# Halving the last image's layer 1 convolution and scores twice

## The chip, the core and the metric

The kernel runs on one core of a Trainium2 chip. The core has a matrix engine (TensorE, "PE" in the profile), a vector engine (VectorE, "DVE"), an activation engine (ScalarE, "ACT"), a general engine (GpSimd, "POOL") and a queue engine that issues most of the transfers (SyncE, "SP"). The metric is the time of one execution on the device in microseconds; a version is measured several times and its median is given.

## What is computed

Two attention layers follow each other on 8 images of 512 channels and 32 x 32 = 1024 tokens, all in float32. The part that matters here is layer 1, which has one head over all 512 channels:

```python
xn = group_norm(x, gamma, beta)
q = conv1x1(xn, q_w, q_b).reshape(b, c, h * w).transpose(0, 2, 1)
k = conv1x1(xn, k_w, k_b).reshape(b, c, h * w)
v = conv1x1(xn, v_w, v_b).reshape(b, c, h * w).transpose(0, 2, 1)
attn = softmax(einsum('bqc,bck->bqk', q, k) * scale, axis=-1)
out = einsum('bqk,bkc->bqc', attn, v).transpose(0, 2, 1).reshape(b, c, h, w)
return x + conv1x1(out, p_w, p_b)
```

Layer 0 has the same form with eight heads of 64 channels. Its output x is layer 1's input.

## The kernel before

**Layer 1 in the kernel.** The query and key weights are multiplied together once, at the start, into a matrix `m`, and the value and output weights into `z`. For an image with normalized input h, the kernel then computes g = m h + `ubias` (a 512 x 512 by 512 x 1024 product, "the convolution"), the scores as the product of h and g (1024 x 1024), the exponentials e of the scores, the sums of e over the keys, z h by token, and the values, z h times e, divided by the sums and added to x.

**Halving.** Each large product is cut into halves in both directions, and the 8 block products are replaced by 7 (the scheme of Strassen in Winograd's form). The blocks to be multiplied are sums and differences of the halves: `left_sums` and `right_sums` make them with 8 half-tile additions each. `wino` runs the seven products in the order 1, four in the middle, then 4 and 3. Each product is a step of four matmuls with 512 columns. The last two steps are not run at once: they go into the list `tail`, and `finish` runs them after the first step of whatever product comes next. So the end of one product and the beginning of the next always overlap on TensorE.

**Halving twice.** For the keys, queries, g and scores of most images each of the seven products is itself cut in halves: 7 x 7 quarter products with 256 columns. `inner_factors` makes the inner sums of h, four GpSimd subtractions for each of the seven (28 in all); `query_factors` does the same for a factor of g (28 in all over the seven); the inner sums of the weights are made once, at the start, by `keep2` and are stored as `sums2_m`. `conv2` runs the convolution in four groups of one or two products (2, 2, 1, 2), `scores1_twice` the scores in seven. Both use `inner_steps` for the seven steps of each: the first step's result is copied inside PSUM by ScalarE, later steps add to it, and VectorE and ScalarE combine the results into output tiles. Where three parts of an output must be added, GpSimd adds them.

**Images in turn.** The main loop runs attention 0 of image b, then products of image b - 1's layer 1 mixed with image b + 1's layer 0. So layer 1 of images 0 to 6 is done inside the loop and is halved twice: there `inner_factors` is called before the projection of image b, well ahead of its use. Layer 1 of image 7 comes after the loop, where nothing of another image is left but the last two steps of image 6's values. It is halved once: `layer1_scores` gets `inner` as None and calls `conv`, and `layer1_rest` calls `scores1`. The normalized h of image 7 is loaded and scaled during image 6's values (the list `ahead`).

**What else hangs on it.** In the loop, group-norm statistics of the image that was just projected (`stats`) are run between the score products, on VectorE. After the loop the list is empty. `scores1` lets VectorE add up e and make the factors of e for the values; `scores1_twice` gives the totals (`add_up`) and the last four of eight subtractions for the values to GpSimd.

**Weights.** Weights are loaded through a pool of three buffers in the order of the list `uses`; `load_weight` issues the next load. A once-halved weight is one load of 1,792 KB; a twice-halved one comes in two, of 1,792 and 1,344 KB. `keep` stores the once-halved sums of a weight to memory (`sums_m` for m), `keep2` the twice-halved ones.

**Order.** Matmuls are pinned to the order of the program, as are some vector operations (`keep_in_program_order`); the rest is placed by a scheduler with its own priorities. Each engine runs its queue in order. Image-sized tiles share one pool of 32 buffers, so a new tile may have to wait for the last reader of an old one.

The names in the profile: `psa_g`, `psb_g`, `psc_g` are PSUM tiles of the convolution; `psa_sc` and the like are those of once-halved scores, and plain `psa`, `psb`, `psc` those of twice-halved ones; `inner_h` are inner sums of h, `inner` those of g, `t_h` and `sg` the outer sums of h and g; `psa_z` and `psa_av` belong to z h and the values.

Of the kernel before, what the change touches and what calls it, by code (L numbers as in the profile page):

```python
# [11 lines left out]
AF = mybir.ActivationFunctionType  # L12
# [3 lines left out]
P = 128  # L16
# [13 lines left out]
def two_attention_blocks_kernel(  # L30
# [145 lines left out]
    def main_path(ctx):  # L176
# [8 lines left out]
        def big_tile(name, shape=(P, T)):  # L185
            return big.tile(list(shape), F32, tag="big", name=name)

        def pair_tile(name):
            return big_tile(name, (P, 2, HT))
# [121 lines left out]
        uses = ["v", "p", *twice["k"], *twice["q"]] if B > 1 else ["p"]  # L311
        for b in range(1, B):
            uses += ["p", *twice["m"], "z"] + (["v", *twice["k"], *twice["q"]] if b + 1 < B else [])
        uses += ["m", "z"]
        loaded = []

        def load_weight():
# [331 lines left out]
            return scaled  # L649


        def scores1(b, gf, hf, uid):

            e = [big_tile(f"e_{uid}_{s}") for s in range(NS)]
            total = pair_tile(f"sum_{uid}")
            flat = total.rearrange("p a b -> p (a b)")
            scale = C**-0.5
            halves = lambda t: (t[:, :HT], t[:, HT:])
            ef = {p: [] for p in range(1, 8)}
            def part(j):  # L660

                def mm(p, i, ps, start):
                    for k in range(2):
                        matmul(
                            ps, hf[p][k][:, ts(2 * j + i, P)], gf[p][k], start=start and k == 0, stop=k == 1, skip_group_check=True
                        )

                def done(i, r, c, ps, u):
                    s = 4 * c + 2 * j + i
                    dst = e[s][:, ts(r, HT)]  # L670
                    if u is None:
                        nc.scalar.activation(dst, ps, AF.Exp, scale=scale)
                    else:
                        nc.vector.tensor_add(dst, ps, u)
                        nc.scalar.activation(dst, dst, AF.Exp, scale=scale)

                    if (r, c) == (1, 0):
                        if s == 0:
                            background.append(lambda: nc.gpsimd.tensor_copy(flat, e[0]))
                        else:  # L680
                            background.append(lambda: nc.vector.tensor_add(flat, flat, e[s]))
                    elif (r, c) == (0, 1):
                        background.append(lambda: nc.vector.tensor_add(flat, flat, e[s]))
                        if i == 1:
                            t = [pair_tile(f"t{n}_{uid}_{j}") for n in (1, 2, 4)]
                            fs, steps = right_sums(
                                [halves(e[2 * j + n]) for n in range(2)], [halves(e[4 + 2 * j + n]) for n in range(2)],
                                [lambda n, t=t: t[:, n, :] for t in t], nc.vector.tensor_sub,
                            )
                            for p in fs:  # L690
                                ef[p] += fs[p]
                            background.extend(steps)


                wino(f"sc_{uid}_{j}", mm, done, middle=(6, 2, 5, 7) if j else (2, 5, 6, 7))

            for j in range(2):
                part(j)
            return total, ef

        def scores1_twice(b, f, gf, gsteps, first, uid, stats):

# [158 lines left out]
        def prologue():  # L861
            raw_k = raw("k", 5)
            raw_q = raw("q", 4)
            h0 = [load_x(0, c, "h0") for c in range(KC)]
            first = {n: prepare(n) for n in "vqk"}
            wk = natural(raw_k, "k", ("a", "b"))
            wq = natural(raw_q, "q", ("c", "acc"))
            norm = GroupNorm(0, "0_0", pinned=True)
            for c in range(KC):
                norm.stats(c, h0[c])  # L870
            hf, steps = image_factors(h0, "h0_0")

# [24 lines left out]
            keep2("k", first["k"][0])  # L897
            t, steps = prepare("m")
            k = conv(weight_factors(first["k"][0]), hf, pcols("bk0"), "k0_0", hooks=[[], [], [], [], steps])
            finish()  # L900
            keep("m", t)
            keep2("m", t)
            raw_p0 = raw("p0", 3)
            wv = natural(raw_v, "v", "bc")
            norm1.group_mean(acc_tile("gmean_0_1")[:, :KC])
            product(wv, raw_p, "z")
            norm1.affine(acc_tile("gvar_0_1")[:, :KC])
            bias = bias_products([(wk, "bq1"), (raw_p, "bv1"), (raw_p0, "bv0")])
# [101 lines left out]
            q = conv2("q", f, pcols("bq0"), f"q0_{b}", hooks)  # L1010
            return q, k

        def layer1_scores(b, hf, inner, hooks=()):
            if inner:
                g = conv2("m", inner, ubias, f"g1_{b}", hooks)
            else:
                after = [load_weight, lambda: background.extend(gsteps)]
                g = conv(weight("m"), hf, ubias, f"g1_{b}", middle=(2, 5, 6, 7), back=4, after=after)
            stiles = [pair_tile(f"sg{i}_{b}") for i in (1, 2, 4)]
            halves = lambda t: (t[:, :HT], t[:, HT:])  # L1020
            gf, gsteps = left_sums(
                [halves(t) for t in g[:2]], [halves(t) for t in g[2:]],
                [lambda j, t=t: t[:, j, :] for t in stiles], nc.vector.tensor_add, nc.vector.tensor_sub,
            )
            return gf, gsteps

        def layer1_rest(b, hf, inner, gf, gsteps, stats, hooks, ahead):
            if inner:
                first = query_factors(gf[1], f"1_1_{b}")
                total, ef = scores1_twice(b, inner, gf, gsteps, first, f"1_{b}", stats)  # L1030
            else:
                total, ef = scores1(b, gf, hf, f"1_{b}")
            state = {}

            def sums():
# [16 lines left out]
        for b in range(B):  # L1052
# [33 lines left out]
            if b > 0:  # L1086
# [2 lines left out]
                for f in sums2:  # L1089
                    f()  # L1090
                norm1, stats = projection(b, af, xt, [scaled, steps[7]])
                gf, gsteps = layer1_scores(b - 1, hf, inner)
                _, _, mean, affine = norm_hooks(norm1, f"1_{b}")
                if b + 1 < B:
                    h, loads, applies = begun(load_x, norm0, b + 1, "h0")
                else:
                    h, loads, applies = begun(load_again, norm1, b, "h1")
                ahead = [loads, *([f] for f in applies)]
                layer1_rest(b - 1, hf, inner, gf, gsteps, stats, [[], mean, [], affine], ahead)
                if b + 1 < B:  # L1100
                    hf, steps = image_factors(h, f"h0_{b + 1}")
                    background.extend(steps)
# [18 lines left out]
                for f in loads + applies:  # L1121
                    f()
        hf, steps = image_factors(h, f"h1_{B - 1}")
        background.extend(steps)
        gf, gsteps = layer1_scores(B - 1, hf, None)
        layer1_rest(B - 1, hf, None, gf, gsteps, [], [[]] * 4, ())
        finish()


# [193 lines left out]
```

## Time and profile before

| | us |
|---|---|
| median of 3 runs | 2852.84 |
| lowest and highest | 2851.77, 2853.81 |
| the profiled execution, its time | 2852.44 |
| the profiled execution, its span | 2850.6 |

| engine | busy us | share of the span |
|---|---|---|
| TensorE, matmul | 2834.5 | 99% |
| TensorE, weight load | 1665.7 | 58% |
| VectorE | 2062.8 | 72% |
| ScalarE | 919.9 | 32% |
| GpSimd | 1106.2 | 39% |

The profile is of one execution. Its span goes from the first to the last instruction; the execution's own time is 1.84 us longer. A line of a timeline gives start and duration in us, engine, line of the code, operation, output tile <- input tiles, shape and the number of records; a float32 matmul of the code leaves two records. Durations of matmuls overlap a little, so the distance between two starts is the better measure. In the stretch from 2684.40 to 2773.69 us, which holds image 7's convolution and scores, TensorE is busy for 89.29 us, VectorE for 46.67, ScalarE for 15.02 and GpSimd for 1.56. In the stretch from 2553.07 to 2628.14, which holds those of image 6, they are busy for 74.88, 56.56, 23.01 and 58.01 us.

### The profile page before, as it was taken

How to read it: one execution, taken by the hardware profiler on the slowest of the kernel's cores; microseconds unless marked ns; L12 is line 12 of the kernel's file. 1: busy time of each engine (PE TensorE's matmuls, PEld its weight loads, DVE VectorE, ACT ScalarE, POOL GpSimd, SP SyncE). 2: the span in 40 equal slices, each digit the busy share in tenths (PEclk: the TensorE clock that was granted, in tenths of full speed). 3: DMA queues.
4: the chain of work that ended last, by engine and by line, in shares of the span. 5: the costliest groups of instructions: out<-in, count | busy, mean ns of one | idle time of the engine just before them, and what ended most of it. 6: DMA issues, size and time to landing. Idle time of an engine off the chain costs nothing.

```text
span 2850.6 us, 32020 instructions
## 1 busy us (share of the span) xinstructions
PE 2834.5 (99%) x11720; PEld 1665.7 (58%) x11720; DVE 2062.8 (72%) x2718; ACT 919.9 (32%) x1166; POOL 1106.2 (39%) x1110
## 2 busy tenths in 40 slices
PE   9999999999999999999999999999999999999999
PEld 5435635866367653677537674376833858348544
DVE  5587787766877678776787757877588775887654
ACT  1252452214522145221552215421163312533110
POOL 2113225732167322673127711377114761147100
PEclk9999999999999999999999999999999999999999
DMA  8722403133032231322213231122411224022201
GB/s 276 246 97 90 179 20 134 37 144 126 20 144 76 100 123 42 118 94 97 112 46 111 93 138 72 49 107 101 154 52 45 107 108 153 16 74 79 96 0 68
DMA packets 91594, 281.02 MB, mean 99 GB/s; under 512 B 10595, under 2 KB 36387, under 8 KB 82470
## 3 DMA queue, kind: packets, MB, share of 16 engines
q1 hardware_dynamic: 89638, 276.61, 26.5%
q10 hardware_dynamic: 1792, 2.29, 0.2%
q8 instruction: 95, 1.56, 0.2%
q14 instruction: 69, 0.57, 0.1%
HBM read 225.93 MB, written 52.93 MB: 98 GB/s over the span
## 4 chain that ended last, share of the span: by engine, by line
PE 98%; issue 1%; DVE 1%; POOL 0%; ACT 0%; DVEq 0%; POOLq 0%
PE sc L67 16%; PE av L67 16%; PE psb_av L67 6%; PE psb L67 5%; PE psa_av L67 4%; PE psc_av L67 4%; PE psc L67 3%; PE psa L67 3%; PE psb_z L67 3%; PE psb_p L67 3%; PE psb_v L67 3%; PE psb_g L67 3%; PE psb_k L67 3%; PE psb_q L67 2%; PE psa_p L67 2%; PE psa_z L67 2%
## 5 line engine op out<-in xcount | busy, mean ns | idle before, releaser
L625 DVE TENSOR_TENSOR sum<-sum,e 128x1024 f32<-128x1024 f32 x384 | 521.0, 1357 | 40.7 <-DVE sum L623 0.5
L621 ACT ACTIVATE e<-sc 128x1024 f32<-128x1024 f32 x512 | 476.8, 1053 | 73.4 <-PE sc L67 72.6
L67 PE MATMUL sc<-q,k 64*128 64x512 f32 x2048 | 458.7, 596 | 0.5
L67 PE MATMUL av<-e,v 128*64 128x512 f32 x2048 | 453.6, 595 | 0.0
L67 PEld LDWEIGHTS sc<-q,k 64*128 64x128 f32 x2048 | 193.2, 186 | 239.2 <-ACT e L621 104.0
L67 PEld LDWEIGHTS av<-e,v 128*64 128x64 f32 x2048 | 141.4, 137 | 304.3 <-issue 304.3
L588 POOL TENSOR_TENSOR all_recs<-all_recs,rc 128x256 f32<-128x256 f32 x72 | 63.5, 882 | 579.6 <-DVE rc L586 572.0
L644 POOL TENSOR_TENSOR a<-a,r 128x512 f32<-128x512 f32 x56 | 108.8, 1943 | 260.8 <-DMA r<-rows 246.5
L586 DVE RECIPROCAL rc<-sums 128x256 f32<-128x256 f32 x72 | 126.4, 1756 | 47.8 <-PE sums L67 26.6
L532 POOL TENSOR_TENSOR k<-k,k 128x256 f32<-128x256 f32 x28 | 20.0, 726 | 314.5 <-DVE u_k L527 314.5
L639 ACT COPY a<-av 128x512 f32<-128x512 f32 x64 | 37.4, 585 | 322.7 <-PE av L67 322.7
L623 DVE TENSOR_TENSOR sum<-e,e 128x1024 f32<-128x1024 f32 x64 | 78.4, 1226 | 59.3 <-ACT e L621 59.3
L67 PE MATMUL psa_av<-e,z 128*128 128x512 f32 x256 | 113.3, 595 | 0.0
L140 ACT ACTIVATE h<-h,b,s 128x1024 f32<-128x1024 f32 x62 | 78.5, 1270 | 87.2 <-DMA h<-in_x 70.6
L67 PE MATMUL psb<-inner,inner_h 128*128 128x256 f32 x392 | 101.6, 382 | 0.8
L411 POOL TENSOR_TENSOR inner_h<-h,inner_h 128x256 f32<-128x256 f32 x112 | 101.1, 905 | 2.2
L67 PEld LDWEIGHTS psb<-inner,inner_h 128*128 128x128 f32 x392 | 73.3, 190 | 14.9 <-POOL inner L426 3.4
L67 PEld LDWEIGHTS psa_av<-e,z 128*128 128x128 f32 x256 | 48.0, 190 | 57.3 <-issue 56.6
L411 POOL TENSOR_TENSOR inner_h<-h 128x256 f32<-128x256 f32 x56 | 55.4, 990 | 66.8 <-ACT h L140 66.8
L411 POOL TENSOR_TENSOR inner_h<-t_h 128x256 f32<-128x256 f32 x84 | 73.6, 879 | 10.8 <-PE psc_av L67 9.5
L67 PE MATMUL psb_g<-inner_h,w_m 128*128 128x256 f32 x294 | 75.1, 383 | 0.3
L67 PE MATMUL psb_q<-inner_h,w_q 128*128 128x256 f32 x294 | 75.4, 385 | 0.0
(382 smaller groups left out, 5435.2 us busy)
## 6 DMA issues: line engine op xcount, KB each, us to landing
x<-in_x SPq DMA_DIRECT2D x36, 512.0 KB
h<-in_x SPq DMA_DIRECT2D x32, 512.0 KB
spill<-x SPq DMA_DIRECT2D x32, 512.0 KB
h<-spill SPq DMA_DIRECT2D x32, 512.0 KB
x<-spill SPq DMA_DIRECT2D x32, 512.0 KB
out<-x SPq DMA_DIRECT2D x64, 256.0 KB
w_p<-sums_p SPq DMA_DIRECT2D x8, 1792.0 KB
r<-rows SPq DMA_DIRECT2D x112, 128.0 KB
```

The costliest lines, as they stand in the source:

```text
L67: tc.keep_in_program_order(nc.tensor.matmul(*args, **kw))
L140: tc.keep_in_program_order(nc.scalar.activation(dst, src, AF.Identity, bias=b, scale=s))
L411: pin(nc.gpsimd.tensor_tensor(dst, x, y, ALU.subtract))
L532: nc.gpsimd.tensor_tensor(d, x, y, ALU.add)
L586: nc.vector.reciprocal(rc, sums)
L588: nc.gpsimd.tensor_tensor(all_recs, all_recs, rc, ALU.add)
L621: nc.scalar.activation(e, sc, AF.Exp, scale=(C // 8) ** -0.5)
L623: nc.vector.tensor_add(total, es[0], e)
L625: nc.vector.tensor_add(total, total, e)
L639: nc.scalar.copy(dst, av)
L644: nc.gpsimd.tensor_tensor(dst, dst, r, ALU.mult)
```

## The change

Image 7's convolution and scores take the twice-halved path, as the other images' do. The once-halved function `scores1` goes, and `scores1_twice` takes its name; `layer1_scores` and `layer1_rest` lose their second branch. After the loop `inner_factors` is called for image 7, its GpSimd operations placed by the scheduler and not pinned, and both the outer and the inner sums of h are called for at once instead of being put in the background list. The list of weight loads has the two parts of m in the place of its once-halved form. The once-halved sums of m are no longer stored, as nobody reads them.

```diff
-        uses += ["m", "z"]
+        uses += [*twice["m"], "z"]
...
-        def scores1(b, gf, hf, uid):
...
-        def scores1_twice(b, f, gf, gsteps, first, uid, stats):
+        def scores1(f, gf, gsteps, first, uid, stats):
...
-            keep("m", t)
             keep2("m", t)
...
-        def layer1_scores(b, hf, inner, hooks=()):
-            if inner:
-                g = conv2("m", inner, ubias, f"g1_{b}", hooks)
-            else:
-                after = [load_weight, lambda: background.extend(gsteps)]
-                g = conv(weight("m"), hf, ubias, f"g1_{b}", middle=(2, 5, 6, 7), back=4, after=after)
+        def layer1_scores(b, inner):
+            g = conv2("m", inner, ubias, f"g1_{b}")
...
-            if inner:
-                first = query_factors(gf[1], f"1_1_{b}")
-                total, ef = scores1_twice(b, inner, gf, gsteps, first, f"1_{b}", stats)
-            else:
-                total, ef = scores1(b, gf, hf, f"1_{b}")
+            first = query_factors(gf[1], f"1_1_{b}")
+            total, ef = scores1(inner, gf, gsteps, first, f"1_{b}", stats)
...
         hf, steps = image_factors(h, f"h1_{B - 1}")
-        background.extend(steps)
-        gf, gsteps = layer1_scores(B - 1, hf, None)
-        layer1_rest(B - 1, hf, None, gf, gsteps, [], [[]] * 4, ())
+        inner, sums2 = inner_factors(hf, f"h1_{B - 1}")
+        for f in steps + sums2:
+            f()
+        gf, gsteps = layer1_scores(B - 1, inner)
+        layer1_rest(B - 1, inner, gf, gsteps, [], [[]] * 4, ())
         finish()
```

More of the change, by code (lines that the diff above doesn't have):

```diff
@@ L649, in attention0 @@
             return scaled
-        def scores1(b, gf, hf, uid):
[L654 to L672, printed above, removed]
-                    else:
[L674 to L679, printed above, removed]
-                        else:
[L681 to L691, printed above, removed]
-                            background.extend(steps)
[L695 to L699, printed above, removed]
-        def scores1_twice(b, f, gf, gsteps, first, uid, stats):
+        def scores1(f, gf, gsteps, first, uid, stats):
             scale = C**-0.5
@@ L1011, in keys_and_queries @@
             return q, k
-        def layer1_scores(b, hf, inner, hooks=()):
-            if inner:
-                g = conv2("m", inner, ubias, f"g1_{b}", hooks)
-            else:
-                after = [load_weight, lambda: background.extend(gsteps)]
-                g = conv(weight("m"), hf, ubias, f"g1_{b}", middle=(2, 5, 6, 7), back=4, after=after)
+        def layer1_scores(b, inner):
+            g = conv2("m", inner, ubias, f"g1_{b}")
             stiles = [pair_tile(f"sg{i}_{b}") for i in (1, 2, 4)]
@@ L1025, in layer1_scores, with layer1_rest @@
             return gf, gsteps
-        def layer1_rest(b, hf, inner, gf, gsteps, stats, hooks, ahead):
-            if inner:
-                first = query_factors(gf[1], f"1_1_{b}")
-                total, ef = scores1_twice(b, inner, gf, gsteps, first, f"1_{b}", stats)
-            else:
-                total, ef = scores1(b, gf, hf, f"1_{b}")
+        def layer1_rest(b, inner, gf, gsteps, stats, hooks, ahead):
+            first = query_factors(gf[1], f"1_1_{b}")
+            total, ef = scores1(inner, gf, gsteps, first, f"1_{b}", stats)
             state = {}
@@ L1091, in main_path @@
                 norm1, stats = projection(b, af, xt, [scaled, steps[7]])
-                gf, gsteps = layer1_scores(b - 1, hf, inner)
+                gf, gsteps = layer1_scores(b - 1, inner)
                 _, _, mean, affine = norm_hooks(norm1, f"1_{b}")
@@ L1098, in main_path @@
                 ahead = [loads, *([f] for f in applies)]
-                layer1_rest(b - 1, hf, inner, gf, gsteps, stats, [[], mean, [], affine], ahead)
+                layer1_rest(b - 1, inner, gf, gsteps, stats, [[], mean, [], affine], ahead)
                 if b + 1 < B:
@@ L1123, in main_path @@
         hf, steps = image_factors(h, f"h1_{B - 1}")
-        background.extend(steps)
-        gf, gsteps = layer1_scores(B - 1, hf, None)
-        layer1_rest(B - 1, hf, None, gf, gsteps, [], [[]] * 4, ())
+        inner, sums2 = inner_factors(hf, f"h1_{B - 1}")
[3 more added lines that the diff above has]
+        layer1_rest(B - 1, inner, gf, gsteps, [], [[]] * 4, ())
         finish()
```

## The prediction

> **What bounds the kernel now.** I read the page first (busy times, then the chain that ended last), then TensorE's timeline over the last image, then the same work for the image before it, which already runs in the changed form, then VectorE and GpSimd at the seam.
>
> ```profile
> span 2850.6 us, 32020 instructions
> PE 2834.5 (99%) x11720; PEld 1665.7 (58%) x11720; DVE 2062.8 (72%) x2718; ACT 919.9 (32%) x1166; POOL 1106.2 (39%) x1110
> ...
> PE 98%; issue 1%; DVE 1%; POOL 0%; ACT 0%; DVEq 0%; POOLq 0%
> ```
>
> TensorE (PE) is busy 99% of the span and is 98% of the chain, at full granted clock. Only fewer or cheaper matmuls can shorten the run, as long as no other engine makes PE wait. So the question is what the last image's stage costs PE now, and what it will cost. Now (timeline of PE; start, duration, tiles, records):
>
> ```profile
> 2684.40 3.60 PE L67 MATMUL psa_g<-h,w_m 128*128 128x512 f32 x8
> 2687.84 7.03 PE L67 MATMUL psb_av<-t,z 128*128 128x512 f32 x16
> 2694.70 7.03 PE L67 MATMUL psc_av<-e,sz 128*128 128x512 f32 x16
> 2701.57 3.60 PE L67 MATMUL psa_g<-h,w_m 128*128 128x512 f32 x8
> ...
> 2763.37 3.62 PE L67 MATMUL psa_z<-w_z,h 128*128 128x256 f32 x16
> ...
> 2773.69 3.62 PE L67 MATMUL psb_z<-w_z,t_h 128*128 128x256 f32 x16
> ```
>
> The convolution and the scores lie between 2684.40 and 2773.69, 89.29 us. Two steps of the previous image's values (7.03 each, 6.87 start to start) and one of z (3.45) lie among them; 89.29 - 13.73 - 3.45 = 72.11 us is the stage itself. Each step is eight records, four matmuls of the code, in 3.433 us: 858 ns for a 128x512 matmul. There are no holes. The image before, in halves twice:
>
> ```profile
> 2553.07 0.59 PE L67 MATMUL psa_g<-h,w_m 128*128 128x256 f32 x2
> ...
> 2626.41 1.03 PE L67 MATMUL psc<-inner,t_h 128*128 128x256 f32 x4
> 2627.27 1.03 PE L67 MATMUL psb<-g,inner_h 128*128 128x256 f32 x4
> 2628.14 3.62 PE L67 MATMUL psb_z<-w_z,t_h 128*128 128x256 f32 x16
> ```
>
> Its steps of two 128x256 matmuls start every 0.863 us (2626.41 to 2627.27; 0.8633 over the regular run around it), so 431.7 ns a matmul. The whole: 75.07 us, less two steps of the projection (6.87) and one of z (3.45), is 64.75 us.
>
> **What the Trainium skill says.** "FP8 and Floating Point Precision", TensorE Precision Notes: true FP32 takes four passes through the array. "TensorE: Matmul & The Clock Gate", Step-by-step: a pass streams one column a cycle at 2.4 GHz plus about 2.5 ns. An estimate from both is 4 x (512/2.4 + 2.5) = 863 ns and 4 x (256/2.4 + 2.5) = 437 ns; the trace has 858 and 432, so splitting a matmul in two costs only some 5 ns, and the product count decides. "SBUF — State Buffer", Who interferes with whom: a VectorE instruction with two SBUF inputs and a GpSimd instruction that reads SBUF exclude each other. The trace agrees: VectorE's 128x512 subtractions take 0.64 us alone (1.28 for two) and 1.17 beside GpSimd (2.34 for two, below).
>
> **Part 1: fewer products.** Removed: 7 products x 4 matmuls for the convolution and 2 x 7 x 4 for the scores, 84 x 0.8584 = 72.11 us. Added: 49 matmuls for the convolution (7 steps x (2+2+1+2) products) and 49 steps x 2 = 98 for the scores, 147 x 0.4317 = 63.45 us. On PE alone: -8.66 us.
>
> **Part 2: what the new hand-overs cost PE.** The image before spent 64.75 us against 63.45 of pure matmul: 1.30 us of waiting, some 0.4 in the convolution (2553.07 to 2582.36, less two projection steps and one score step, is 21.56; 49 matmuls are 21.15) and 0.9 in the scores. The latter sits at 2590.99 to 2599.65, where VectorE had run three group-norm statistics (1.87 us from 2583.42) ahead of the sums of g, and GpSimd stood 2.56 us for `sg` before it could make the third product's inner sums. The last image has no next image's statistics (its list is empty), so those sums come about 2 us sooner. I keep the 0.4 us and take 0.3 for the scores: +0.7. Bounds: 0 (all hidden) and 1.3 (as before it).
>
> **Part 3: the inner sums of h (28 GpSimd operations) and the seam.** They are new, ahead of everything else in GpSimd's queue, and stand in the previous image's values, where GpSimd is idle now after 2652. h is ready at 2663.6 to 2667.4. 28 x 0.9 us (the mean of those groups on the page is 879 to 990 ns) is 25 us, so they end near 2691; their tiles' old readers are all among values matmuls that end by 2677. The convolution's first use of an inner sum follows the two values steps, at 2684.40 + 0.86 + 13.73 = 2699.0. 8 us of cover: cost 0; without it, each us late is a us of PE. The eight VectorE sums of h run beside them now, each up to 0.53 us longer, and behind them stands `u_av`, whose end PE needs at 2677.54 (it ends at 2674.99 now, after 2.10 us of idleness). The same collision exists already, where an image's layer 0 sums meet the previous values (timelines of VectorE, PE and GpSimd):
>
> ```profile
> 2324.22 2.34 DVE L172 TENSOR_TENSOR h<-h,h 128x512 f32<-128x512 f32 x2
> 2326.49 2.34 DVE L173 TENSOR_TENSOR t_h<-h,t_h 128x512 f32<-128x512 f32 x2
> 2328.75 0.68 DVE L238 TENSOR_TENSOR u_av<-psb_av,t_av 128x512 f32<-128x512 f32 x1
> ...
> 2329.96 7.03 PE L67 MATMUL psb_av<-e,z 128*128 128x512 f32 x16
> 2342.12 1.52 POOL L411 TENSOR_TENSOR inner_h<-t_h,inner_h 128x256 f32<-128x256 f32 x2
> ```
>
> `u_av` ends at 2329.43, 0.5 us ahead of the matmul that needs it, and PE runs on. There h came 5.56 us after the second psa_av step began, here 5.43. So 0, with 0.5 us of slack; bounds 0 and 2.2 (13 two-input operations x 0.53 = 6.9, less the 4.65 us in hand: VectorE is free at 2672.20, and a start at 2676.85 is early enough).
>
> **Part 4: after the scores.** Twice-halved scores hand the totals, and four of the value sums, to GpSimd. The image before has this too: its total is done at 2636.5, PE asks for it at 2642.5; its last value sum at 2652.1, wanted at 2687.8. From psb_z to the end of the corresponding values steps PE took 56.26 us there and takes 55.82 here; the difference is the two group-norm matmuls, which the last image lacks. The closing check of the reciprocals now waits for GpSimd's last value sums and has z's additions queued behind it on VectorE; I place it some 2.6 us ahead of the first of these. Cost 0, bounds 0 and 1.
>
> **Part 5: memory traffic.** One 1,792 KB store of the once-halved m goes from the start; the last image's m comes in two loads (1,792 and 1,344 KB) and z's weight one load later, after the old z weight's last use (2656.9) and needed at 2763. On SP's queue the store's absence moves the load of v's weight ahead of image 1's h loads, so these have as many bytes before them as now (1,792 KB less, 1,792 more) and go out about 3 us later. ScalarE applied the first at 129.19 without waiting and has until about 133.6 (the copy at 134.91 less 1.30). Nothing else that PE reads early depends on it. Cost 0, bounds 0 and 1.
>
> **Sum.** -8.66 + 0.7 = -7.96 us. Against the profiled execution (2852.44: span 2850.6 and 1.84 around it) that is 2844.5; the median of the runs shown lies 0.4 above that execution, so 2844.9.
>
> **The rivals.**
> A, the forecast: PE keeps nearly all of the saving. For it: 98% of the chain and no holes in either form. 2844.9, its own range 2843.5 to 2846.2 (waits of 0 to 1.3, and about 0.7 us of scatter).
> B, waits between engines take a larger part: the last image stalls like the one before (1.3) and loses as much again, because the next matmul of each product waits for a ScalarE copy or a VectorE sum of the one just ended. For: each product needs PE, ScalarE, VectorE in turn. Against: the other images bear more load with 1.3. -8.66 + 2.6 = -6.1: 2846.8.
> C, the collision at the seam: the price above, 2.2, plus the 0.7: -5.8: 2847.0; a late h would add to it, to 2849.
> D, slower: the load of v's weight, ahead of h on a saturated queue (240 to 440 GB/s from 97 to 145 us), delays h, and ScalarE, which runs in order, holds the next exponentials. Every us past 133.6 is lost; it must arrive after 141.5 to make the kernel slower at all, after 147 for 0.2%. An arrival at 147 gives 133.6 to 147 less the saving, 5.5 us more: 2858. Against: the byte count ahead is unchanged.
> That the saving isn't there at all is excluded by the instruction order, which has the 147 matmuls.
>
> **How the numbers follow.** A 0.71, B 0.17, C 0.09, D 0.03. One measurement of this kernel can tell about 0.2%, 5.7 us, from no change: faster means below 2847.1. A gives all its 0.71, B about 0.11, C 0.02: 0.84. D gives 0.03 slower; 0.13 is left within. The range 2843.0 to 2848.2 holds A, B and most of C; what is left out is D, the late h in C, and scatter.
>
> **What would show it.** Right: g and score steps of 128x256 at 0.863 us, 64 us of stage, the z step's psb_z some 8 us earlier than 2773.69, the rest displaced by the same. Part 2 is wrong if the stage takes 65.5 or more; part 3 if PE has a hole before psb_av<-e,z near 2677 or before the first psb_g near 2699; part 4 if there is one before sums or the psa_av steps of the last image; part 5 if the first scores of the run shift. The forecast falls if the stage's saving and the span's differ by over 1 us.

## The result, and the profile after

| | before | after |
|---|---|---|
| median, us (20 runs each) | 2852.68 | 2848.70 |
| lowest and highest | 2851.47, 2854.32 | 2847.18, 2849.99 |
| profiled execution, its span | 2852.44, 2850.6 | 2849.52, 2847.7 |
| ratio, 95% interval | | 0.9984, 0.9978 to 0.9991 |

The changed kernel is 4.0 us faster, where 7.9 were forecast. The gain is real (the interval ends below 1), but small: 0.14% by the medians, 0.16% by the ratio, below the 0.2% that I had named as what one measurement can tell. 2848.70 lies 0.5 us above the range.

The page of the changed kernel, first its span and engines, then the engines' shares of the chain that ended last:

```profile
span 2847.7 us, 32456 instructions
PE 2827.0 (99%) x11846; PEld 1690.0 (59%) x11846; DVE 2083.8 (73%) x2733; ACT 929.0 (33%) x1177; POOL 1205.4 (42%) x1193
...
PE 97%; DVE 2%; issue 1%; ACT 0%; POOL 0%; DVEq 0%; POOLq 0%; ACTq 0%
```

PE has 7.5 us less to do (2834.5 to 2827.0), the span only 2.9. PE's busy time says that the saving is there; the rest of the page doesn't say where it went. PE's timeline over the last image does:

```profile
2686.92 0.59 PE L67 MATMUL psa_g<-h,w_m 128*128 128x256 f32 x2
...
2701.52 1.03 PE L67 MATMUL psb_g<-inner_h,w_m 128*128 128x256 f32 x4
...
2727.34 1.03 PE L67 MATMUL psc<-inner,h 128*128 128x256 f32 x4
2728.83 1.13 PE L67 MATMUL psb<-g,inner_h 128*128 128x256 f32 x4 [0.47 <-DVE e L671]
2729.80 1.03 PE L67 MATMUL psb<-inner,inner_h 128*128 128x256 f32 x4
```

And where it ends, from the same view:

```profile
2768.81 3.62 PE L67 MATMUL psb_z<-w_z,t_h 128*128 128x256 f32 x16
```

Three things are to be read here. The stage takes 81.89 us from psa_g to psb_z; less the same two values steps and one z step (17.18) it is 64.71 where the kernel before had 72.11: 7.40 saved. But psa_g starts at 2686.92, 2.52 us *later* than before (2684.40): something was lost ahead of the change. And psb_z starts 4.88 us earlier, while the span is only 2.9 shorter: 2 us more were lost behind it. I laid the starts of all of PE's rows in both traces side by side. They drift apart in steps, where PE stops in one trace and not in the other: by 0.79 at 179 us, by 1.06 at 955, by 0.36 at 1200, and by some 0.1 at each of three later places. Behind the stage PE keeps its 4.88 us to its last matmul; the rest goes between VectorE's last operation and the end of the span, 4.95 us before and 6.93 after.

### The profile page after: what moved, and what is told of

It reads as the page before. It is cut to its first block, busy times and chain, and to the rows that moved or that the text cites. A ratio compares the mean times of both kernels' runs of the same rounds, so it can differ in the third digit from the quotient of the medians.

```text
span 2847.7 us, 32456 instructions
## 1 busy us (share of the span) xinstructions
PE 2827.0 (99%) x11846; PEld 1690.0 (59%) x11846; DVE 2083.8 (73%) x2733; ACT 929.0 (33%) x1177; POOL 1205.4 (42%) x1193
## 4 chain that ended last, share of the span: by engine, by line
PE 97%; DVE 2%; issue 1%; ACT 0%; POOL 0%; DVEq 0%; POOLq 0%; ACTq 0%
PE sc L67 16%; PE av L67 16%; PE psb_av L67 6%; PE psb L67 5%; PE psa_av L67 4%; PE psc_av L67 4%; PE psc L67 3%; PE psa L67 3%; PE psb_z L67 3%; PE psb_p L67 3%; PE psb_v L67 3%; PE psb_k L67 3%; PE psb_g L67 3%; PE psb_q L67 2%; PE psa_p L67 2%; PE psa_z L67 2%
## 5 line engine op out<-in xcount | busy, mean ns | idle before, releaser
L67 PE MATMUL psb<-inner,inner_h 128*128 128x256 f32 x448 | 116.1, 382 | 1.2 <-DVE u L671 0.5
L411 POOL TENSOR_TENSOR inner_h<-h,inner_h 128x256 f32<-128x256 f32 x120 | 106.8, 892 | 2.2
L67 PEld LDWEIGHTS psb<-inner,inner_h 128*128 128x128 f32 x448 | 83.9, 190 | 16.9 <-POOL inner L426 3.8
L685 POOL TENSOR_TENSOR sum<-sum,e 128x1024 f32<-128x1024 f32 x32 | 76.2, 2380 | 27.5 <-ACT e L681 26.2
L67 PE MATMUL psb_g<-inner_h,w_m 128*128 128x256 f32 x336 | 86.0, 383 | 0.3
```

The source lines that it names most:

```text
L67: tc.keep_in_program_order(nc.tensor.matmul(*args, **kw))
L411: pin(nc.gpsimd.tensor_tensor(dst, x, y, ALU.subtract))
L685: on = lambda dst, x, y: lambda: tc.keep_in_program_order(nc.gpsimd.tensor_tensor(dst, x, y, ALU.add))
```

## What happened at the start

PE's waits in the first 260 us have one line that the kernel before hasn't:

```profile
PE sums L67 <- DVE sum L625: 0.7, 1, 0.7
```

SP's timeline, before the change (start, time in the queue's hands, DMA):

```profile
117.77 0.37 SPq L840 DMA_DIRECT2D product_z<-prodz  x1
118.69 1.67 SPq L282 DMA_DIRECT2D prepare_z<-product_z  x2
120.42 0.56 SPq L209 DMA_DIRECT2D h<-in_x  x1
...
125.03 0.46 SPq L209 DMA_DIRECT2D h<-in_x  x1
126.05 1.46 SPq L858 DMA_DIRECT2D bias_cols<-bias_rows_dram  x3
127.55 0.98 SPq L209 DMA_DIRECT2D h<-in_x  x2
128.57 0.43 SPq L328 DMA_DIRECT2D w_v<-sums_v  x1
...
142.06 1.37 SPq L600 DMA_DIRECT2D r<-rows  x2
```

and after it:

```profile
114.24 0.49 SPq L791 DMA_DIRECT2D product_z<-prodz  x1
121.06 0.87 SPq L282 DMA_DIRECT2D prepare_z<-product_z  x2
121.98 0.46 SPq L328 DMA_DIRECT2D w_v<-sums_v  x1
122.54 0.38 SPq L791 DMA_DIRECT2D product_z<-prodz  x1
...
123.91 1.35 SPq L209 DMA_DIRECT2D h<-in_x  x1
133.43 0.38 SPq L282 DMA_DIRECT2D prepare_z<-product_z  x1
...
136.01 1.43 SPq L209 DMA_DIRECT2D h<-in_x  x3
...
149.43 1.46 SPq L600 DMA_DIRECT2D r<-rows  x2
```

Two lines of SP's own waits in the stretch from 105 to 155 us (total, times, longest) say where SP stood. They name the transfer to be issued by its line, and what it waited for. Before:

```profile
SPq L328 <- DMA sums_p<-prepare_p: 3.5, 1, 3.5
SPq L282 <- DMA product_z<-prodz: 2.7, 2, 2.2
```

and after:

```profile
SPq L282 <- DMA product_z<-prodz: 14.3, 2, 8.1
SPq L328 <- DMA sums_p<-prepare_p: 10.3, 1, 10.3
```

L328 is the load of a weight's sums, L282 the reading back of z's product. (The letter q in a name like SPq stands for the part of the engine that reads its instructions and issues transfers.) Each must wait until the store of what it reads has landed (arrived in memory), and SP runs its queue in order, so everything behind it waits too.

What ScalarE and GpSimd waited for, before:

```profile
129.19 1.30 ACT L140 ACTIVATE h<-h,b,s 128x1024 f32<-128x1024 f32 x1
149.77 1.60 POOL L644 TENSOR_TENSOR a<-a,r 128x512 f32<-128x512 f32 x1 [11.29 <-DMA r<-rows]
```

and after:

```profile
134.70 1.24 ACT L140 ACTIVATE h<-h,b,s 128x1024 f32<-128x1024 f32 x1 [5.30 <-DMA h<-in_x]
158.47 1.28 POOL L644 TENSOR_TENSOR a<-a,r 128x512 f32<-128x512 f32 x1 [19.96 <-DVE sum L625]
```

Three loads have to be told apart.

- **The first load of h** still goes out ahead of the long waits, right behind v's weight: at 123.91 instead of 120.42. ScalarE stood 5.30 us for it and applied it at 134.70 instead of 129.19, 5.5 us later and past the 133.6 that the prediction had as the limit. But its next exponential came at 136.56, where it had come at 136.54: the slack was just used up.
- **The other three loads of h** stand behind the second store of z's product and its reading back. SP waits 8.1 us for that store's landing, until 133.43, and these loads go out from 136.0 on, 9 to 11 us later than before.
- **The load of p's weight** comes next. The sums that it reads were themselves stored behind those h loads (at 137.54, before at 135.68), and SP waits 10.3 us for their landing, before 3.5. So p's weight goes out at 149.01 instead of 141.65, and `r` right behind it at 149.43 instead of 142.06.

What did reach PE was the late `r`. GpSimd's scaling of `a`, which needs it, came at 158.5 instead of 149.8 (the last part of its wait the profile puts down to a sum on VectorE), and later ones fell beside VectorE's sums of the exponentials, whose six took 9.98 us instead of 8.76. VectorE went on to its next operation 1.6 us later than before (179.42 instead of 177.83), and PE, which needs the last of the sums, waited 0.72 us at 179. The steps of this chain are read from one trace; experiments 2 and 3 test it, by bringing `r` forward.

## The experiments

"End" below is the time from the end of VectorE's last operation (the last x, start plus 0.75) to the end of the span. "Stage" is from the last image's first psa_g to its psb_z, less 17.18. A "stop" is a place where PE waits; the stop of 1.04 us is the one seen at 955.

**1. The changed kernel again**, no edit.

> The changed kernel once more, unaltered. Theory S (the late loads of the start are built into the order of SP's queue): PE's wait at the fourth sums of the first attention (0.72 us) is there again, and the copy of image 7's first psa_g starts again some 2 us or more after 2684.40, where the kernel before has it. Theory N (the time between the start and the last image is scatter from one execution to the next): the first psa_g of the last image starts within 0.5 us of 2684.40, or at any rate somewhere else than 2686.92. The long VectorE multiplication in image 1's values (7.81 us) and the 2 us longer end behind the last matmul should be there again only if they belong to the kernel; if they come from chance they are gone. Time 2848.7, between 2847.2 and 2850.0.

2848.46 (2846.96 to 2849.78). In its profile psa_g starts at 2686.62, the waits of 0.73 (sums) and 0.8 us (beside the 7.8 us multiplication) are back, the stage is 64.71, the end 7.23. So what was lost at these places is not the scatter of one execution.

**2. The store put back.**

```diff
             finish()
+            keep("m", t)
             keep2("m", t)
```

> The changed kernel with the 1,792 KB store of the once-halved m put back (nobody reads it). SP's queue then has the order of the kernel before, all other engines that of the changed one. Theory S: image 1's first h arrives before 129.2, its w_p load goes out near 141.7 and not 149.0, the 0.72 us wait at the fourth sums goes, the last image starts at 2684.4 to 2685.5, and the time falls to 2846 to 2847. Theory N: no change, 2848.7.

2847.92 (2845.82 to 2849.22). The 0.72 us wait is gone, `r` goes out at 143.5, h is applied at 128.44, psa_g starts at 2684.70: theory S holds for the start of the trace. psa_g's start alone mixes other things in: the stop of 1.04 us, which the first profile of before lacks, and the start of PE's first work, ps_wm, at 10.66 (11.42 in that profile; in all of them 10.3 to 11.9). From PE's first work to psa_g, without the stop, it is 2673.0 us, as before, and 1.3 less than in the changed kernel. The time missed its expectation: against experiment 1 it fell by 0.5 us (interval -2.1 to +0.2), not to 2847 or below. Its end of 7.55 us took part of it; so the 1.3 us of the start are seen in the traces, and not clear of noise in the medians.

**3. v's weight held behind h.**

```diff
-            nc.sync.dma_start(t, x[b, c * P : (c + 1) * P, :])
+            load = nc.sync.dma_start(t, x[b, c * P : (c + 1) * P, :])
+            if (b, what) == (1, "h0"):
+                tc.keep_in_program_order(load)
...
-                    nc.sync.dma_start(t, wdram[n])
+                    load = nc.sync.dma_start(t, wdram[n])
+                    if not loaded:
+                        tc.keep_in_program_order(load)
```

> The changed kernel without the store, but with image 1's h loads and the load of v's weight held in the order of the code, so that v's weight comes after them on SP's queue; the second product_z store is no longer behind it either. Theory S: the same as with the store put back, h there before 129, no 0.72 us wait, 2846 to 2847. If instead the store's absence itself (less traffic, other pairs of collisions later) made the loss: as the changed kernel, 2848.7.

2848.15 (2847.32 to 2849.54). The 0.72 us wait is gone here too, with no store: the order on SP's queue made it, not the traffic. This time too missed its expectation (0.3 us less than experiment 1, interval -0.7 to +0.3). Short stops in images 2 to 6 remain (0.35 at 1200, 0.28 at 1548 and three of 0.1 to 0.16); the changed kernel has such stops too (0.36 at 1200, then 0.1 three times), experiment 2 has one, of 0.1. The stop at 1200 is in all seven profiles that have another order of SP's queue than the kernel before (the changed kernel and experiments 1, 3, 4, 8, 9, 10) and in none of the seven that have its order. So it goes with that order; by what way is open.

**4. The sums of g held behind the sums PE waits for**, on top of 3.

```diff
+            pin = tc.keep_in_program_order if uid == f"1_{B - 1}" else lambda ins: ins
...
-                nc.vector.tensor_add(dst[0], ps, x[0])
+                pin(nc.vector.tensor_add(dst[0], ps, x[0]))
...
-                [lambda j, t=t: t[:, j, :] for t in stiles], nc.vector.tensor_add, nc.vector.tensor_sub,
+                [lambda j, t=t: t[:, j, :] for t in stiles],
+                lambda *a: pin(nc.vector.tensor_add(*a)), lambda *a: pin(nc.vector.tensor_sub(*a)),
```

> As the run with the pinned loads, and in the last image VectorE's sums of g are held in the order of the code behind the sums that PE's banks wait for: the in-place subtractions of g (2.35 us beside GpSimd) no longer stand ahead of the addition that frees psb. Theory: PE's hole of 0.63 us at the eighth score step goes and the scores of the last image lose some 0.2 instead of 0.9 us, 0.6 us less than the pinned loads alone. Rival: the subtractions come late for the third product's inner sums on GpSimd, and the hole only moves or grows: no gain, up to 1 us more.

2847.40 (2845.89 to 2848.91), stage 64.09: 0.62 us less than in 3, as expected. VectorE around the place of the hole, in the changed kernel:

```profile
2725.83 2.35 DVE L161 TENSOR_TENSOR g<-g 128x512 f32<-128x512 f32 x2
2728.10 0.68 DVE L671 TENSOR_TENSOR e<-psb,c 128x512 f32<-128x512 f32 x1
```

and here:

```profile
2722.48 1.81 DVE L976 TENSOR_TENSOR sg<-g,g 128x512 f32<-128x512 f32 x2
2725.14 0.69 DVE L676 TENSOR_TENSOR e<-psb,c 128x512 f32<-128x512 f32 x1 [0.85 <-PE psb L67]
2726.79 0.69 DVE L676 TENSOR_TENSOR e<-psc,u 128x512 f32<-128x512 f32 x1 [0.96 <-PE psc L67]
```

In the changed kernel the addition that empties the PSUM tile psb, so that PE can write it again, stands behind two subtractions of g; here it starts when its operand comes, and PE runs on.

**5. The kernel before again**, no edit.

> The kernel before once more, unaltered, for a second profile. In the first, PE goes through image 1's values without a stop, and 4.95 us lie between the end of VectorE's last operation and the end of the span; the five profiles of the changed kernel and its variants have a 1.04 us stop there (VectorE's 7.81 us multiplication beside GpSimd) and 6.93 to 7.55 us at the end. Theory C (both are properties of the changed program): again no stop near 948, again 4.9 to 5.2 us at the end. Rival R (the first profile was a lucky one): the stop of 1.0 us near 948 is in this profile too, or the end has 7 us.

2852.60 (2851.37 to 2854.45). No stop near 948, end 4.75. For the end theory C holds. For the stop it seemed to, and didn't: see experiments 9 to 11.

**6. Only the scores halved twice**, with the store put back. It forms the sums of g twice on VectorE (once in the convolution's tail, once among the scores), which changes g.

```diff
-        uses += [*twice["m"], "z"]
+        uses += ["m", "z"]
...
+                after = [load_weight, lambda: background.extend(gsteps)]
+                g = conv(weight("m"), hf, ubias, f"g1_{b}", middle=(2, 5, 6, 7), back=4, after=after)
```

> The last image's scores in halves twice, its convolution in halves once (28 matmuls of 128x512 on one load of the once-halved m, which is stored at the start as in the run with the store put back). On PE the convolution costs 28 x 0.8584 = 24.0 us in place of 21.5, so the time is 2.5 us above the run with the store put back: 2850.4. If the convolution's three engines in turn had cost more than 0.4 us of waiting, the difference would be smaller. The end behind VectorE's last operation: 6.9 to 7.6 us if it is a property of the last image's new scores and values; anything from 5 to 7.5 if it depends on where PE's stream of instructions ends, which is shorter here.

2849.92 (2848.62 to 2851.36), stage 69.30: the eight operations too many on VectorE made PE wait some 3 us in the scores. That tells nothing about the convolution, but how little VectorE has to spare at this place. End 5.08. That the time lies near the expected 2850.4 is luck: the stage took more than expected, the end less.

**7. Only the convolution halved twice**, with the store put back and the former once-halved scores.

```diff
+            keep("m", t)
...
-            total, ef = scores1(inner, gf, gsteps, first, f"1_{b}", stats)
+            if last is None:
+                first = query_factors(gf[1], f"1_1_{b}")
+                total, ef = scores1(inner, gf, gsteps, first, f"1_{b}", stats)
+            else:
+                total, ef = scores1_once(b, gf, last, f"1_{b}")
```

> The last image's convolution in halves twice, its scores in halves once (56 matmuls of 128x512), with the store of the once-halved m put back so that the start is the kernel before's. Scores cost 48.1 us in place of 43.2 (42.3 of matmuls and 0.9 of waiting), so 4.9 us above the run with the store put back: 2852.8; if the waits in the scores are not what the trace says, 5.8 or 4. The end behind VectorE's last operation: 5 us if the twice-halved scores make it long, anything from 5 to 7.5 if it depends on where PE's stream of instructions ends.

2851.22 (2850.14 to 2854.43), stage 70.02: 21.15 of matmuls and 0.35 of waiting for the convolution, 48.07 and 0.45 for the scores. The 3.3 us over experiment 2 are 5.3 in the stage less 2.1 at the end (5.44), with no stop of 1.04 us here.

**8. Sixteen small matmuls at the start of PE's stream**, on top of 4.

```diff
+            for h in range(2):
+                warm = acc_tile(f"warm{h}")
+                for _ in range(8):
+                    matmul(warm[0:1, 0:1], ones[:, 0:1], ones[:, 0:1], start=True, stop=True)
```

> The run with the pinned loads and the pinned sums of g, and 16 one-column matmuls of ones ahead of everything else on PE, while PE waits for the first weights: no time, but PE's instructions all lie further on in its stream. If the end of 6.9 to 7.6 us depends on where PE's stream ends, it changes (5 us if this place suits, then 2845.2 in place of 2847.4); if it belongs to the work of the last image, it stays, and so does 2847.4.

2845.72 (2843.74 to 2847.05), end 4.76: 2.5 us less at the end than in 4, and 1.7 less in the time (interval 0.5 to 2.9), by work that does nothing. Its profile also lacks the stop of 1.04 us that 4's has.

**9. The same sixteen in the changed kernel alone.**

> The changed kernel with nothing else than 16 one-column matmuls of ones ahead of everything on PE, in the time in which PE waits for the first weights. Theory P (the 2 us at the end come from where PE's instruction stream ends, and the stop of 1.04 us in image 1's values hangs on small shifts): the end behind VectorE's last operation is 4.7 to 5.1 us, SP's wait for PE's sequencer 0.5 us in place of 2.1, the stop may be there or not; the 0.72 us wait at the start stays. Time 2848.5 less 2.0 to 3.2: 2845.3 to 2846.5. Rival: the matmuls helped only together with the pinned loads and sums, the end stays at 7 us: 2848.5.

2845.89 (2844.67 to 2847.55), end 4.93. The waits of SP at the end of the run, in the changed kernel:

```profile
SPq L1264 <- PEq L1264: 2.6, 2, 2.1
```

in the kernel before:

```profile
SPq L1319 <- PEq L1319: 0.6, 2, 0.5
```

and here:

```profile
SPq L1268 <- PEq L1268: 0.6, 2, 0.5
```

PEq is PE's sequencer, which reads PE's instructions, and the line is the program's end, past the jump over the general path (code that runs only when the closing check fails). Nothing that PE computes stands there. PE's own instructions at that line (in ns the shortest, median and longest of each, then when the first and the last started) show where the time goes. Before:

```profile
L1279 PEldq COMPARE_BRANCH  x1: 3652/3652/3652, 2844.8 to 2844.8; - x1
L1279 PEldq EVENT_SEMAPHORE  x1: 51/51/51, 2848.5 to 2848.5; - x1
L1319 PEldq DRAIN  x2: 8/8/8, 2848.7 to 2850.2; - x2
```

and in the changed kernel:

```profile
L1224 PEldq COMPARE_BRANCH  x1: 3607/3607/3607, 2839.9 to 2839.9; - x1
L1224 PEldq EVENT_SEMAPHORE  x1: 51/51/51, 2843.6 to 2843.6; - x1
L1264 PEldq DRAIN  x2: 8/8/8, 2847.0 to 2847.3; - x2
```

The jump itself (COMPARE_BRANCH) takes as long in both. What differs is the step from the first instruction past it to the next one: from 2848.5 to 2848.7 before, from 2843.6 to 2847.0 here. That step takes 3.1 to 3.6 us in the five profiles with a long end and 0.15 to 0.2 in the nine others. Sixteen more matmuls in the code ahead take it away: 2.6 us less in the time than in experiment 1 (interval 1.8 to 3.5). All 0.72 us of the wait at the start are still there.

**10. Forty of them.** As 9, with 20 in place of 8.

> The same with 40 such matmuls, so that the stream ends elsewhere again. Theory P: again another end, between 4.7 and 7.5 us; if the end is 4.7 to 5.1 us at most places and 7 us at a few only, 2845.3 to 2846.5. Rival as for 16: 2848.5.

2847.84 (2846.25 to 2849.26), end 5.16. The end is short again, as theory P has it, but the time is only 0.6 us below experiment 1, and 1.95 above experiment 9 (interval 1.1 to 2.7), from which it differs by 24 matmuls and 0.23 us at the end. In the profile PE's first work, ps_wm, began at 11.71, where experiment 9 has 10.66. That explains little, as the two profiles of the unaltered kernel before differ as much, 11.42 and 10.68. Theory P doesn't cover this difference, and it stays open.

**11. Six of them in the kernel before.**

> The kernel before with 6 such matmuls ahead of everything on PE, about as many instructions as the changed kernel's stream is longer by, counted modulo 256. Theory P: if 256 instructions is the unit in which PE's stream is fetched, the end is 6.9 to 7.6 us in place of 4.9 and the time 2854.7; if the unit is another, the end may be anything from 4.7 to 7.5. Rival (the longer end belongs to the last image's new work): 4.9 us, 2852.7.

2851.98 (2851.23 to 2853.37), end 5.39. The end isn't long, as it would have been had 256 instructions been the unit and the place right. But 256 was a supposition of mine that no run shows, and this run decides little about it: PE's stream is 277 instructions longer in the changed kernel's trace than before, 21 more than 256, and here it is 24 longer. The late step at the end lies between two neighbouring instructions, so three instructions may be enough to miss it. I have no run in which the kernel before ends late.

The profile also has a stop of 1.04 us in image 4's values, at 1999, the same as that at 955 in the changed kernel; experiment 9 has two (images 1 and 5), experiment 10 one (image 3). So theory C is wrong about the stop: the work of the kernel before can have it too. At 955 it is in six of the eleven profiles with the changed last image or half of it. Experiment 8 differs from 4, which has it, only by the 16 matmuls. How often each kernel has it is open, so up to a microsecond of the measured difference can be due to it.

**12. Only the scores halved twice, the sums of g formed once.** The lines are against experiment 6.

```diff
-                after = [load_weight, lambda: background.extend(gsteps)]
-                g = conv(weight("m"), hf, ubias, f"g1_{b}", middle=(2, 5, 6, 7), back=4, after=after)
+                g = conv(weight("m"), hf, ubias, f"g1_{b}", middle=(2, 5, 6, 7), back=4, after=[load_weight])
```

> The last image's scores in halves twice and its convolution in halves once, with the store of the once-halved m put back, as in the sixth run, but with the sums of g formed once and not twice. On PE: the convolution's 24.0 us in place of 21.5; its end of PE's stream is near that of the sixth run, so the end is 5.1 us. Stage from the first psa_g to psb_z, less two values steps and one z step: 24.0 + 43.2 = 67.2 us. Time: that with the store put back (2847.9) plus 2.5 less 2.2 for the end: 2848.2.

2847.39 (2846.27 to 2848.50), stage 66.51: 24.03 and 42.31 of matmuls and 0.16 of waiting. With the convolution halved once, the scores wait 0.16 us instead of 0.89. So the second halving of the convolution, worth 2.9 us of matmuls (24.03 - 21.15), brings 1.8: 0.36 goes to its own hand-overs and 0.73 to those of the scores. In the medians this half of the change is 1.1 us faster than the whole: its end is shorter (5.18), and it has the former order of SP's queue. Against experiment 2, which has that order too, it is 0.5 us faster (interval -1.3 to +1.0), which is not clear of noise.

**All profiles together.** The column "sum" below puts each profile's difference from the kernel before together from three parts:

- the stage, less 72.11;
- the end, less 4.85 (the mean of experiment 5's and the first profile's);
- the start and images 0 to 6, from the first ps_wm to the last image's psa_g, stops of 1.04 us taken out. This is 2673.0 to 2673.2 with the former order of SP's queue (six profiles beside that of before), 2674.2 to 2674.5 with the changed order (four), and 2673.7 to 2673.9 with the pinned loads (three), so I take 0, +1.3 and +0.8.

"Measured" is the median less that of the runs of before beside it.

| kernel | stops of 1.04 | stage | end | sum | measured |
|---|---|---|---|---|---|
| changed | 1 | 64.71 | 6.93 | -4.0 | -4.0 |
| 1, again | 1 | 64.71 | 7.23 | -3.7 | -4.3 |
| 2, store put back | 1 | 64.71 | 7.55 | -4.7 | -4.8 |
| 3, loads pinned | 1 | 64.71 | 6.98 | -4.5 | -4.6 |
| 4, and sums of g pinned | 1 | 64.09 | 7.26 | -4.8 | -5.4 |
| 6, scores only, sums twice | 0 | 69.30 | 5.08 | -2.6 | -2.7 |
| 7, convolution only | 0 | 70.02 | 5.44 | -1.5 | -1.4 |
| 8, as 4, 16 matmuls | 0 | 64.09 | 4.76 | -7.3 | -6.9 |
| 9, changed, 16 matmuls | 2 | 64.71 | 4.93 | -6.0 | -6.7 |
| 10, changed, 40 matmuls | 1 | 64.71 | 5.16 | -5.8 | -4.8 |
| 11, before, 6 matmuls | 1 | 72.10 | 5.39 | +0.5 | -0.7 |
| 12, scores only | 0 | 66.51 | 5.18 | -5.3 | -5.2 |

The sums meet the medians within 0.7 us but for experiments 10 and 11, each off by 1.0 to 1.2, which stay unexplained. As the stops are left out of them, a sum that is met exactly, as in the first row, is partly luck: with its stop counted, the first profile of the changed kernel is 2.9 us shorter than that of before, as the spans are. The five profiles with the changed kernel's stream on PE end with 6.93 to 7.55 us, whatever the other queues do; the nine with another stream, of either kernel, with 4.75 to 5.44.

The version with the pinned loads, the pinned sums of g and the 16 matmuls (experiment 8) beats the kernel before, 0.9975 of its time (0.9965 to 0.9985). The 16 matmuls alone (experiment 9) do as well, 0.9976 (0.9967 to 0.9985), so what the pins add doesn't show beside them.

## Why the prediction was off

By its own sign of failure (the stage's saving and the span's differ by over 1 us) the forecast fell: 7.40 against 2.9, or 4.0 in the medians.

- **Part 1, right.** The steps of 128x256 start every 0.863 us; 63.45 us of matmuls are in the stage, 64.71 with waits.
- **Part 2, half right.** The convolution's 0.4 us was 0.36. For the scores I took 0.3 instead of the previous image's 0.9, "The last image has no next image's statistics"; they lost 0.89. The statistics weren't what held them: two subtractions of g, each some 1.2 us beside GpSimd, stand ahead of the addition that empties psb for PE (experiment 4 moves them and gets 0.62 back). Mis-sized by 0.56, within its bound of 1.3.
- **Part 3, right.** No hole before psb_av<-e,z (2680.06, 2.52 later like everything) nor before psb_g at 2701.52: the inner sums of h and the collision at the seam cost nothing, and rival C is out.
- **Part 4, right as far as it went.** From psb_z to the start of the second to last values step, 2824.63, it is 55.82 us as before.
- **Part 5, wrong.** I saw that v's weight moved ahead of h, counted the bytes ahead of h as equal and wrote "go out about 3 us later", "Nothing else that PE reads early depends on it" and "Cost 0, bounds 0 and 1". The first h load did go out 3.5 us later, but right behind v's weight, and it was applied 5.5 us later. And the count passed over what else moved: the second store of z's product went behind the weight, and its reading back ahead of h's other three loads. An instruction that waits at the head of SP's queue holds all behind it, whatever the bytes: 8.1 us here, and 10.3 at the next one, the load of p's weight. It cost PE 0.72 us in one wait, and about 1.3 with the small stops that come with this order; both are read in the traces, not in medians. It was rival D's beginning. ScalarE's slack took all of the lateness of h, which came past D's 133.6 without holding the next exponential. PE was reached by another way than D's, the load of `r`, which I hadn't looked at.
- **The sum, wrong by a term it didn't have.** It took the 1.84 us around the span and the tail within it as fixed. The end grew by 2.1 us (6.93 against 4.85). It goes with PE's stream of instructions: 16 matmuls that compute nothing of use take it away (experiments 8 and 9). Why the changed kernel's stream ends late is open. Nothing in the profile of before foretells this; a bound for it would have had to come from other programs, and the twelve runs put it at 0 to 2.7.

-7.96 + 0.56 + 1.3 + 2.1 is -4.0, the measured difference. The stop of 1.04 us is not in this sum, and other kernels' sums miss by up to 1.2, so the exact meeting is partly luck. Rivals B (2846.8, more waiting between engines in the stage) and C (2847.0, the seam) were nearer in number, for reasons that weren't the main ones.

## What to carry to other kernels

When a change frees a place in a DMA queue, read the new order of the whole queue and look for instructions that wait at its head, above all for a store that is read back; equal bytes do not mean equal arrival, and the first engine to suffer may be another than the one whose load moved. A gain of 0.3% in one stage is of the size of things that have nothing to do with it: compare the starts of the same instructions along both traces, and the time behind the last one, before crediting or blaming the stage. And a slack found "just enough" in one trace (here from 129.19 to about 133.6) should be priced, not counted as zero.

## What the runs showed of the hardware

**The end depends on PE's stream.** 16 one-column matmuls, hidden in PE's wait for its first data, took 2.0 to 2.5 us off the end in two kernels. The late piece is a single step, between two neighbouring instructions of PE past its last jump, of 3.1 to 3.6 us or of 0.15 to 0.2. What PE waits for there no run shows.

**VectorE and GpSimd can shut each other out for 7 us.** GpSimd in experiment 2, at the stop:

```profile
923.30 1.24 POOL L411 TENSOR_TENSOR inner_h<-h 128x256 f32<-128x256 f32 x1 [10.90 <-ACT h L140]
925.40 7.02 POOL L411 TENSOR_TENSOR inner_h<-h,h 128x256 f32<-128x256 f32 x1 [0.86 <-ACT h L140]
932.38 0.72 POOL L411 TENSOR_TENSOR inner_h<-h,inner_h 128x256 f32<-128x256 f32 x1
```

VectorE a little later, in the same run:

```profile
942.25 7.81 DVE L746 TENSOR_TENSOR o<-o,r 128x512 f32<-128x512 f32 x1
```

and GpSimd in experiment 8, without the stop:

```profile
923.19 0.90 POOL L415 TENSOR_TENSOR inner_h<-h 128x256 f32<-128x256 f32 x1 [11.24 <-PE psa_av L67]
924.53 0.76 POOL L415 TENSOR_TENSOR inner_h<-h,h 128x256 f32<-128x256 f32 x1 [0.44 <-ACT h L140]
925.24 1.18 POOL L415 TENSOR_TENSOR inner_h<-h,inner_h 128x256 f32<-128x256 f32 x1
```

Usually both slow down and alternate (1.17 us each, as the prediction used). But where GpSimd had stood 0.86 us for its h before its second sum began at 925.40, that sum came through only when VectorE had finished its whole run of two-input additions at full speed (1.28 for two), and then VectorE's multiplication stood 7.81 us while GpSimd ran through its sums at 0.72 each. GpSimd's spans are rough, as the Trainium skill warns ("Perfetto Trace Analysis", GPSIMD Engine Instruction: go by the spacing of starts); here the spacing says the same, 6.98 us from 925.40 to 932.38. The skill's "SBUF — State Buffer", Who interferes with whom, calls the shared port an exclusive lock; these lines agree, and show that its turns need not alternate. It cost PE 1.04 us each time, in images 1, 3, 4 or 5. In all nine such stops of the kept traces GpSimd had stood 0.61 to 0.99 us for h's second tile, and its sum then took 6.9 to 7.3 us; in the 86 other places of the same kind it had stood 0.00 to 0.62 us, and the sum took 0.73 to 1.24. What makes h's second tile late is open: in experiment 2 ScalarE, which makes it, had itself waited 0.86 us for that tile's load, in experiment 9 it had not.
